# First chunk's copies on ScalarE and its keys turned ahead of the queries' product; VectorE scales queries ahead of the settling

## The chip, the cores and the metric

The kernel runs on one core of a Trainium2 chip. The metric is device time in microseconds; lower is better. A core has TensorE (matrix products, PE in the profile), VectorE (DVE), ScalarE (ACT), GpSimd (POOL) and SyncE (SP). Each engine works through its own queue in order. TensorE's results land in PSUM, eight banks of 128 x 512 float32.

## The reference, cut to what matters

A block with layer norm, an attention that has a sparse and a local part, and a small product with rounded operands, on a batch of 4 sequences of 1024 tokens of 512 channels, 16 heads of 128:

```
xn  = layernorm(x)
q   = rope(rmsnorm(xn @ Wq + bq));  lk = rope(rmsnorm(xn @ Wlk + blk));  lv = xn @ Wlv + blv
ck, cv = compressed keys and values: each 4 tokens pooled by softmax(xn @ Wcmp), then @ Wk, @ Wv
sparse: softmax over the top 8 of the causal q.ck, times cv
local:  softmax over q.lk of this window of 128 and the one before, times lv
out = x + (0.5 * (sparse + local)) @ Wo + bo + fp8(xn) @ fp8(input2) rescaled
```

All of the attention is float32.

## The kernel before, in words

A chunk is 128 tokens (one window); there are 32 chunks, `t` = 0 to 31, eight to a batch element (c = 0 to 7). A unit is two heads of a chunk: eight units to a chunk, `u` = 0 to 7, and 256 units in all. One loop goes over stages, `for s in range(-3, NN + 2)`, and each stage works on several units at once, as a pipeline written out by hand; the order of the calls in the loop is the order of the instructions in every engine's queue (the schedule is manual). In stage `s`:

- `scores(s)`: TensorE, local and sparse scores of both heads into two PSUM banks (`sc`).
- `keep_context(s-2)`: ScalarE copies the context out of PSUM (`cT`, L779).
- `weigh(s)`: VectorE finds the minimum, the top 8 and marks them (L649 to L655), ScalarE takes the exponentials (L656, L664).
- `queries(s+3)`: TensorE, the product for queries and local keys of a unit (`qp`, L478), two banks.
- `turn_keys_here(s+1)`: TensorE turns scaled queries and keys (`tq`, L534), only in the first chunk. Later chunks turn them by VectorE transposes and DMAs through memory (`turn_keys`, L556, L559, L564, and `fetch_keys`, L574).
- `settle(s)`: VectorE zeroes what is not in the top 8 and divides (L671, L680, L681, L682). `settle_window(s)`: ScalarE divides the local part (L687).
- `normalize(s+2)`: VectorE scales queries and keys out of PSUM (`th`, L506), GpSimd and VectorE begin the rotary embedding (`rotate`: `rb`, L332 on GpSimd, and L333 on VectorE). `end_rotation(s+2)` finishes it (L335, L336).
- `turn(s)` and `fetch(s)`: the probabilities are transposed on VectorE (L705), written to memory (L713) and read back turned (`probT`, L747). In the first chunk and for the last unit TensorE turns them instead (`turn_here`, L728) and `keep_turned` copies them out of PSUM (L736).
- `squares(s+3)` on ScalarE (L318) and `spread(s+3)` on GpSimd (L312, L313: the factor `r` that `normalize` of the next stage needs).
- `keep_keys(s+1)`: in the first chunk, copies `tq` to `qT` (L540) and `lkT` (L541).
- `to_output(s-2)` (L797), `values_of(s+1)` (`vp`, L581), `values(s-1)` (`cp`, L764): TensorE. `keep_values(s+1)`: ScalarE copies `vp` to `lv` (L593).

Between these stand `steps()`, twice a stage: pieces of `chunk_prep(t+2)` (layer norm, `xn`, its transposes `xp`, copies `xnT`, the product `yp`, the compressed entries `ep`, `kv`, their rotation `rb_e`, `ckT`) and of `chunk_eight(t)` (rounding of the chunk, L284 to L295, and its product `fp`).

Only in the first chunk: at the end of stages 0 to 7 `fold_first_row(s)` changes a unit's query weights in place on VectorE (`wqk`, L269) after a DMA (`load_first_row`), stages 0 to 3 also round `w2` on VectorE and GpSimd (`round_w2`), and ScalarE's queue issues DMAs for weights.

SyncE's queue issues, in each later stage: the write of the probabilities, four writes of the keys (L564, after L559), four reads of the turned probabilities (L747), two reads of the turned keys (L574). Two PSUM banks, tag `pp`, are used in turn by `tq`, `vp`, `tp` and the tiles of the chunk's preparation (`xp`, `yp`, `ep`, `cp` for `ckT`, `fp`), so a new tile waits until the one before the last has been copied out.

Of the kernel before, what the change touches and what calls it, by code (L numbers as in the profile page):

```python
# [12 lines left out]
F32 = mybir.dt.float32  # L13
BF16 = mybir.dt.bfloat16
U32 = mybir.dt.uint32
AF = mybir.ActivationFunctionType
ALU = mybir.AluOpType
AX = mybir.AxisListType

P = 128  # L20
# [18 lines left out]
def kernel(  # L39
# [26 lines left out]
    nc = tc.nc  # L66
    B, S, HID = hidden.shape
# [10 lines left out]
    work = ctx.enter_context(tc.tile_pool(name="work", bufs=2))  # L78
# [7 lines left out]
    def scratch(name, shape=(P, 512), dtype=F32):  # L86
        return work.tile(list(shape), dtype, tag="scratch", name=name, bufs=2)

    def pp(name):
        return psum.tile([P, 512], F32, tag="pp", name=name, bufs=2)  # L90
# [229 lines left out]
    def rotate(th, cs, nh, a, name):  # L320

        p = th.shape[0]
        a = a.rearrange("p (h t f) -> p h t f", h=nh, t=2)
        bb = work.tile([p, nh, 2, HALF], F32, tag=f"ropeb{nh}", name=f"rb_{name}", bufs=1)
        x12 = th[:, :, 0:ROPE].rearrange("p h (t f) -> p h t f", t=2)

        def wide(v):
            return v.unsqueeze(1).unsqueeze(1).to_broadcast([p, nh, 2, HALF])  # L330

        nc.gpsimd.tensor_tensor(bb, x12, wide(cs[:, HALF:ROPE]), ALU.mult)  # L332
        nc.vector.tensor_tensor(a, x12, wide(cs[:, 0:HALF]), ALU.mult)  # L333
        yield
        nc.vector.tensor_tensor(x12[:, :, 0, :], a[:, :, 0, :], bb[:, :, 1, :], ALU.subtract)  # L335
        nc.vector.tensor_tensor(x12[:, :, 1, :], a[:, :, 1, :], bb[:, :, 0, :], ALU.add)  # L336
# [5 lines left out]
    def chunk_prep(t):  # L342

        b, c = divmod(t, NCH)
        xt = x_tiles.pop(("norm", t))
        if c == 0:
            entries[b] = (
                work.tile([P, 2 * P], F32, tag="ckT", name=f"ckT_{b}"),
                work.tile([P, 2, D], F32, tag="cv", name=f"cv_{b}"),
            )  # L350
        ckT, cv = entries[b]
        st = work.tile([P, 8], F32, tag="lnst", name=f"lnst_{t}")
        nc.vector.bn_stats(st[:, 0:6], xt)
        nc.vector.bn_aggr(st[:, 6:8], st[:, 0:6])
        r = rstd_of(st[:, 7:8], 1, 1.0, EPS_LN, f"lnr_{t}")
        yield "A0"
        if c == 0:
            nc.gpsimd.memset(cv, 0.0)
        yield "B0"

        off = work.tile([P, 2], F32, tag="off", name=f"off_{t}")
        nc.gpsimd.tensor_scalar(off[:, 0:1], st[:, 6:7], -1.0, None, ALU.mult)
        nc.scalar.activation(
            xt, xt, AF.Identity, bias=off[:, 0:1], scale=1.0, accum_out=off[:, 1:2]
        )
        nc.gpsimd.tensor_scalar(off[:, 1:2], off[:, 1:2], 1.0 / HID, None, ALU.mult)
        yield "A1"
        xn = scratch(f"xn_{t}")
        nc.vector.tensor_scalar(xn, xt, off[:, 1:2], r, ALU.subtract, ALU.mult)
        yield "B1"  # L370
        xp = pp(f"xp_{t}")
        for k in range(KK):
            nc.tensor.transpose(xp[:, ts(k, P)], xn[:, ts(k, P)], ident)  # L373
        yield "A2"
        xnT = work.tile([P, KK + 1, P], F32, tag="xnT", name=f"xnT_{t}")
        nc.scalar.copy(xnT[:, 0:KK, :].rearrange("p k s -> p (k s)"), xp)
        if t:
            nc.scalar.copy(xnT[:, KK, :], xp[:, 0:P])
            nc.vector.memset(xnT[0:1, KK, :], 1.0)
        chunks[t] = xnT  # L380
        yield "B2"


        yp = pp(f"yp_{t}")
        for k in range(KK):
            nc.tensor.matmul(  # L386
                yp[:, 0 : 2 * D + 1],
                xnT[:, k, :],
                wkv_sb[:, k, :],
                start=(k == 0),  # L390
                stop=(k == KK - 1),
            )
        yield "A3"
        y = scratch(f"y_{t}")[:, 0 : 2 * D + 1]
        nc.scalar.copy(y[:, 0 : 2 * D], yp[:, 0 : 2 * D])
        nc.gpsimd.memset(y[:, 2 * D : 2 * D + 1], 1.0)
        nc.vector.tensor_scalar(
            logits[:, 0:1], yp[:, 2 * D : 2 * D + 1], bcmp_sb, None, ALU.add
        )
        row = work.tile([P, 2, BLK], F32, tag="row", name=f"row_{t}", bufs=1)  # L400
        red = work.tile([P, BLK // RATIO], F32, tag="red", name=f"red_{t}", bufs=1)
        nc.vector.transpose(row[:, 0, :], logits)
        fours = row[:, 0, :].rearrange("p (n r) -> p n r", r=RATIO)
        nc.vector.tensor_reduce(red, fours, AX.X, ALU.max)
        nc.vector.tensor_tensor(
            fours, fours, red.unsqueeze(2).to_broadcast([P, BLK // RATIO, RATIO]), ALU.subtract
        )
        nc.scalar.activation(row[:, 0, :], row[:, 0, :], AF.Exp)
        yield "B3"
        yield "A4"  # L410
        spread_w = work.tile([P, NE], F32, tag="spread", name=f"spread_{t}", bufs=1)
        nc.vector.transpose(row[:, 1, :], row[:, 0, :])
        nc.vector.tensor_scalar(spread_w, picks, row[:, 1, 0:1], None, ALU.mult)
        yield "B4"
        ep = pp(f"ep_{t}")
        nc.tensor.matmul(ep[0:NE, 0 : 2 * D + 1], spread_w, y, start=True, stop=True)  # L416
        yield "A5"
        total = work.tile([NE, 1], F32, tag="total", name=f"total_{t}", bufs=1)
        kv = work.tile([NE, 2, D], F32, tag="kv", name=f"kv_{t}", bufs=1)
        nc.vector.reciprocal(total, ep[0:NE, 2 * D : 2 * D + 1])  # L420
        nc.vector.scalar_tensor_tensor(
            kv.rearrange("p h d -> p (h d)"),
            ep[0:NE, 0 : 2 * D],
            total,
            bkv_sb,
            ALU.mult,
            ALU.add,
        )
        yield "B5"
        g, o = divmod(c * NE, P)  # L430
        nc.scalar.copy(cv[o : o + NE, g, :], kv[:, 1, :])
        ess = work.tile([NE, 1], F32, tag="ess", name=f"ess_{t}", bufs=1)
        square_sum(ess, kv[:, 0, :], f"e{t}")
        er = rstd_of(ess, 1, 1.0 / D, EPS_RMS, f"er_{t}")
        ck = kv[:, 0:1, :]
        yield "A6"
        nc.vector.scalar_tensor_tensor(
            ck[:, 0, :], ck[:, 0, :], er, norm_w[0:NE, 1, :], ALU.mult, ALU.mult
        )
        ra = work.tile([NE, ROPE], F32, tag="ra_e", name=f"ra_e{t}", bufs=1)  # L440
        for _ in rotate(ck, angles[t][1], 1, ra, f"e{t}"):
            pass
        yield "B6"
        cp = pp(f"cp_{t}")
        nc.tensor.transpose(cp[:, 0:NE], ck[:, 0, :], ident[:NE, :NE])  # L445
        yield "A7"
        nc.vector.tensor_copy(ckT[:, ts(c, NE)], cp[:, 0:NE])
        yield "B7"
# [18 lines left out]
    units = {}  # L467
# [33 lines left out]
    def normalize(n):  # L501
# [15 lines left out]
        next(w["rotation"])  # L517
        w["th"], w["thb"] = th, thb

    def end_rotation(n):  # L520
        for _ in units[n].pop("rotation"):
            pass
# [13 lines left out]
    def keep_keys(n):  # L536
        w = units[n]
        tq = w.pop("tq").rearrange("p (t g a i) -> p t g a i", t=2, g=2, a=NB)
        qT, lkT = key_tiles(n)
        nc.scalar.copy(qT.rearrange("p a (i g) -> p g a i", g=2), tq[:, 0])  # L540
        nc.vector.tensor_copy(lkT.rearrange("p a (g i) -> p g a i", g=2), tq[:, 1])  # L541

    def key_tiles(n):
        w = units[n]
# [144 lines left out]
    def parts_of(n):  # L689

        c, m, _, _ = columns(n)
        return range(0 if c else 1, 3 if m <= P else 4)
# [38 lines left out]
    def keep_turned(n):  # L731
        w, g = units[n], len(parts_of(n))
        probT = work.tile([P, 1024], F32, tag="probT", name=f"probT_{n}", bufs=1)
        probT = of_heads(probT, n)
        for h, tp in enumerate(w.pop("tp")):
            (nc.vector.tensor_copy if h else nc.scalar.copy)(  # L736
                probT[:, :, ds(h * g, g), :],
                tp.rearrange("p (g a i) -> p a g i", a=NB, i=BLK),
            )
        w["probT"] = probT  # L740
# [81 lines left out]
    def for_unit(n, *todo):  # L822
        if 0 <= n < NN:
            for f, *more in todo:
                f(n, *more)
# [9 lines left out]
    for s in range(-3, NN + 2):  # L835
        t, u = place(s)
# [10 lines left out]
        for_unit(s, (scores, 0), (scores, 1))  # L847
        for_unit(s - 2, (keep_context,))
        for_unit(s, (weigh, 0), (weigh, 1))
        for_unit(s + 3, (queries,))  # L850
        if s + 1 < NU:
            for_unit(s + 1, (turn_keys_here,))
        for_unit(s, (settle, 0), (settle, 1))
        for_unit(s, (settle_window, 0), (settle_window, 1))
        for_unit(s + 2, (normalize,))
        if by_dma(s):
            turn(s)
        if s < 0:
# [92 lines left out]
```

## Time and profile before

| | |
|---|---|
| median of 4 runs | 2797.93 us (2797.27 to 2799.34) |
| the profiled execution: time, span | 2797.12 us, 2795.4 us |
| TensorE busy | 2732.9 us (98%) |
| VectorE busy | 2264.9 us (81%) |
| ScalarE busy | 1345.2 us (48%) |
| GpSimd busy | 843.1 us (30%) |
| first scores of unit 0, 1, ... 8 at | 45.13, 59.29, 76.78, 91.42, 109.88, 125.31, 137.56, 149.51, 158.72 us |

All times are from one profiled execution, in microseconds from the start of its span. A line of the timeline gives the start, the time, the engine, the line of the kernel, the operation, what it writes and reads, shapes, a count, and in brackets how long the engine stood idle before it and what ended that. A line of the waits gives who waited for whom, the total, how many times, and the longest. TensorE's clock is the granted one, 1.00 for full.

The stages of the first chunk (from one unit's first scores to the next's) take 9.2 to 18.5 us; those of the later chunks take 8.8 to 12.4 us.

### The profile page before, as it was taken

The page shows a single profiled execution, that of the slowest core. Times are in us where ns is not written, and L with a number is a line of the kernel's source. Part 1 is how long each engine was busy: PE and PEld are TensorE (multiplying, and loading weights), DVE is VectorE, ACT ScalarE, POOL GpSimd, SP SyncE. Part 2 cuts the span into 40 slices and gives each one's busy share as a digit, 9 for nine tenths or more (in the row PEclk, how much of TensorE's full clock was granted, in tenths as well). Part 3 has the DMA queues.
Part 4 walks back from the last instruction along what each step waited for, and adds up shares of the span by engine and source line. Part 5 has one row for each costly group of instructions (what it writes and reads, how often), then busy time and mean ns, then how long its engine had stood idle before and what let it go on. Part 6 is the DMA issues. An engine that isn't in the chain of part 4 may idle for free.

```text
span 2795.4 us, 48431 instructions
## 1 busy us (share of the span) xinstructions
PE 2732.9 (98%) x12686; PEld 1855.6 (66%) x12721; DVE 2264.9 (81%) x9171; ACT 1345.2 (48%) x5170; POOL 843.1 (30%) x1225
## 2 busy tenths in 40 slices
PE   5799999999999999999999999999999999999998
PEld 3566666676666666666666666666666666676665
DVE  4687888888877788888887787888888878888887
ACT  2344554544455554444445555444444555444543
POOL 2333332233232333322233322333223333222331
PEclk8899999999999999999999999999999999999999
DMA  6244445555544445555554444555555444455554
GB/s 203 93 124 138 135 137 152 159 152 152 148 126 141 139 137 143 151 154 155 148 144 132 134 139 138 154 154 144 153 150 142 128 138 140 135 155 161 147 148 128
DMA packets 623187, 401.96 MB, mean 144 GB/s; under 512 B 307152, under 2 KB 576320, under 8 KB 622912
## 3 DMA queue, kind: packets, MB, share of 16 engines
q1 hardware_dynamic: 610688, 385.29, 49.7%
q10 hardware_dynamic: 12224, 13.56, 1.5%
q8 instruction: 104, 1.70, 0.3%
q14 instruction: 171, 1.40, 0.2%
HBM read 214.64 MB, written 184.03 MB: 143 GB/s over the span
## 4 chain that ended last, share of the span: by engine, by line
PE 93%; DVE 2%; DMA 0%; issue 0%; ACT 0%; SPq 0%; POOL 0%; DVEq 0%; ACTq 0%
PE qp L478 31%; PE op L797 15%; PE vp L581 15%; PE cp L764 14%; PE sc L626 5%; PE sc L616 4%; PE sc L623 4%; PE yp L386 2%; PE fp L458 1%; PE ep L416 1%; PE xp L373 0%; DVE wqk L269 0%; PE sc L627 0%; DMA probT<-pr 0%; PE cp L445 0%
## 5 line engine op out<-in xcount | busy, mean ns | idle before, releaser
L478 PE MATMUL qp<-wqk,xnT 128*128 128x512 f32 x2048 | 945.4, 604 | 2.8 <-issue 2.1
L332 POOL TENSOR_TENSOR rb<-th,cs 128x256 f32<-128x256 f32 x256 | 248.5, 971 | 1674.7 <-DVE th L506 1674.7
L478 PEld LDWEIGHTS qp<-wqk,xnT 128*128 128x128 f32 x2048 | 370.6, 191 | 383.4 <-issue 372.3
L581 PEld LDWEIGHTS vp<-wlv,xnT 128*128 128x128 f32 x2048 | 393.0, 192 | 181.2 <-issue 115.3
L581 PE MATMUL vp<-wlv,xnT 128*128 128x256 f32 x2048 | 491.3, 383 | 17.5 <-DVE lkT L541 13.6
L656 ACT ACTIVATE prob<-sc,neg 128x256 f32<-128x256 f32 (+1 forms) x512 | 235.5, 460 | 553.6 <-DVE taken L655 543.9
L797 PE MATMUL op<-wo,cT 128*128 128x512 f32 x1024 | 488.0, 599 | 0.5 <-ACT cT L779 0.5
L649 DVE CUSTOM_DVE_ANT_0 sc<-sc,mask_b 128x256 f32<-128x256 f32 (+1 forms) x512 | 208.4, 407 | 277.9 <-PE sc L627 277.7
L593 ACT COPY lv<-vp 128x256 f32<-128x256 f32 x256 | 95.2, 372 | 469.7 <-PE cp L764 410.7
L687 ACT ACTIVATE prob<-prob,tot 128x256 f32<-128x256 f32 (+1 forms) x512 | 252.4, 493 | 129.0 <-DVE tot L681 127.7
L797 PEld LDWEIGHTS op<-wo,cT 128*128 128x128 f32 x1024 | 186.4, 190 | 189.4 <-issue 128.0
L764 PE MATMUL cp<-probT,lv 128*128 128x128 f32 x1920 | 299.8, 276 | 6.1 <-DMA probT<-pr 5.3
L318 ACT ACTIVATE junk<-qp 128x128 bf16<-128x128 f32 x1024 | 279.7, 273 | 33.0 <-PE qp L478 4.9
L506 DVE SCALAR_TENSOR_TENSOR th<-qp,r,norm_w 128x128 f32<-128x128 f32 x1024 | 287.0, 343 | 7.4 <-PE tq L534 4.1
L764 PEld LDWEIGHTS cp<-probT,lv 128*128 128x128 f32 x1920 | 274.7, 192 | 22.7 <-issue 10.5
L705 DVE STREAM_TRANSPOSE probB<-prob 128x512 f32<-128x512 f32 (+2 forms) x494 | 282.2, 609 | 0.0
L313 POOL TENSOR_TENSOR r<-r,nhalf 128x4 f32<-128x4 f32 x256 | 260.6, 1018 | 21.3
L764 PE MATMUL cp<-probT,cv 128*128 128x128 f32 x1536 | 256.6, 276 | 0.0
L626 PE MATMUL sc<-ckT,qT 128*128 128x96 f32 (+7 forms) x1024 | 226.5, 303 | 0.0
L764 PEld LDWEIGHTS cp<-probT,cv 128*128 128x128 f32 x1536 | 214.1, 193 | 0.0
L623 PE MATMUL sc<-lkT,qT 128*128 128x128 f32 x1024 | 208.1, 285 | 0.0
L779 ACT ACTIVATE cT<-cp,blvT 128x128 f32<-128x128 f32 x512 | 160.0, 364 | 91.6 <-PE cp L764 82.3
(130 smaller groups left out, 3797.0 us busy)
## 6 DMA issues: line engine op xcount, KB each, us to landing
pr<-probB SPq DMA_DIRECT2D x127, 512.0 KB, 2.6
probT<-pr SPq DMA_DIRECT2D x508, 128.0 KB, 2.9
qk<-thb SPq DMA_DIRECT2D x992, 64.0 KB, 1.8
pr<-probB SPq DMA_DIRECT2D x96, 384.0 KB, 2.3
probT<-pr SPq DMA_DIRECT2D x384, 96.0 KB, 2.3
qT<-qk SPq DMA_DIRECT2D x248, 128.0 KB, 2.9
lkT<-qk SPq DMA_DIRECT2D x248, 128.0 KB, 2.7
x_norm<-_attn_hidden_states_dram SPq DMA_DIRECT2D x32, 256.0 KB, 3.2
```

The lines of the kernel that those rows point to most:

```text
L313: nc.gpsimd.tensor_tensor(r, r, nhalf[: ss.shape[0], 0:n], ALU.pow)
L318: nc.scalar.activation(junk[: src.shape[0]], src, AF.Square, accum_out=acc)
L332: nc.gpsimd.tensor_tensor(bb, x12, wide(cs[:, HALF:ROPE]), ALU.mult)
L478: nc.tensor.matmul(qp, xnT[:, k if k or not t else KK, :], wqk_sb[u][:, k, :], start=(k == 0), stop=(t > 0 and k == KK - 1),)
L506: nc.vector.scalar_tensor_tensor(th[:, i, :], qp[:, ts(i, D)], r[:, i : i + 1], norm_w[:, i // 2, :], ALU.mult, ALU.mult,)
L581: nc.tensor.matmul(vp[:, 0:256], xnT[:, k, :], wlv_sb[u][:, k, :], start=(k == 0), stop=(k == KK - 1),)
L623: nc.tensor.matmul(blocks(sc[:, P : 2 * P]), q, lkT[:, :, ds(h * BLK, BLK)], start=True, stop=True)
L626: nc.tensor.matmul(sc[:, spa], q, ckT[:, 0:m], start=True, stop=False)
L687: nc.scalar.mul(prob[:, loc], prob[:, loc], tot[:, 0:1])
L705: nc.vector.transpose(pb[:, :, ds(h * g, g), :], prob[:, parts[0] * P : (parts[-1] + 1) * P].rearrange("p (g b i) -> p b g i", b=NB, i=BLK),)
L764: nc.tensor.matmul(blocks(cp[:, h, :]), v, probT[:, :, h * len(parts) + i - parts[0], :], start=(i == parts[0]), stop=(i == parts[-1]),)
L797: nc.tensor.matmul(op, cT[:, h, :], wo_sb[u][:, h, :], start=(u == 0 and h == 0), stop=(u == NU - 1 and h == 1),)
```

## The change

Six edits:

1. `chunk_prep(0)` no longer centres the chunk on ScalarE; VectorE subtracts the mean of the statistics directly. Later chunks keep the centring.
2. `rotate` yields once more, between GpSimd's and VectorE's first products, and a new call `go_on_rotating` continues it.
3. `keep_keys`: the copy to `lkT` goes from VectorE to ScalarE.
4. `keep_turned`: the second head's copy goes from VectorE to ScalarE.
5. `turn_keys_here(s+1)` goes ahead of `queries(s+3)`.
6. `normalize(s+2)` (scaling and GpSimd's part of the rotation) goes ahead of `settle(s)`, and VectorE's first part of the rotation stays behind `settle_window(s)`.

```diff
@@ rotate
         nc.gpsimd.tensor_tensor(bb, x12, wide(cs[:, HALF:ROPE]), ALU.mult)
+        yield
         nc.vector.tensor_tensor(a, x12, wide(cs[:, 0:HALF]), ALU.mult)
         yield
@@ chunk_prep
-        off = work.tile([P, 2], F32, tag="off", name=f"off_{t}")
-        nc.gpsimd.tensor_scalar(off[:, 0:1], st[:, 6:7], -1.0, None, ALU.mult)
-        nc.scalar.activation(
-            xt, xt, AF.Identity, bias=off[:, 0:1], scale=1.0, accum_out=off[:, 1:2]
-        )
-        nc.gpsimd.tensor_scalar(off[:, 1:2], off[:, 1:2], 1.0 / HID, None, ALU.mult)
+        xn = None
+        if t:
...
+        else:
+            xn = scratch(f"xn_{t}")
+            nc.vector.tensor_scalar(xn, xt, st[:, 6:7], r, ALU.subtract, ALU.mult)
         yield "A1"
-        xn = scratch(f"xn_{t}")
-        nc.vector.tensor_scalar(xn, xt, off[:, 1:2], r, ALU.subtract, ALU.mult)
+        if t:
+            xn = scratch(f"xn_{t}")
+            nc.vector.tensor_scalar(xn, xt, off[:, 1:2], r, ALU.subtract, ALU.mult)
         yield "B1"
@@
+    def go_on_rotating(n):
+        next(units[n]["rotation"])
+
@@ keep_keys
-        nc.vector.tensor_copy(lkT.rearrange("p a (g i) -> p g a i", g=2), tq[:, 1])
+        nc.scalar.copy(lkT.rearrange("p a (g i) -> p g a i", g=2), tq[:, 1])
@@ keep_turned
-            (nc.vector.tensor_copy if h else nc.scalar.copy)(
+            nc.scalar.copy(
@@ the loop over stages
         for_unit(s, (weigh, 0), (weigh, 1))
-        for_unit(s + 3, (queries,))
         if s + 1 < NU:
             for_unit(s + 1, (turn_keys_here,))
+        for_unit(s + 3, (queries,))
+        for_unit(s + 2, (normalize,))
         for_unit(s, (settle, 0), (settle, 1))
         for_unit(s, (settle_window, 0), (settle_window, 1))
-        for_unit(s + 2, (normalize,))
+        for_unit(s + 2, (go_on_rotating,))
         if by_dma(s):
             turn(s)
```

## The prediction

> **What bounds the kernel now.** I read the busy times by stretch first, then the waits of each engine inside and outside the first chunk, then the timeline of single stages.
>
> ```profile
> 45.00:159.00 114.00, 88.67 (x370) 59.98 (x373) 79.96 (x286) 39.51 (x171) 40.62 (x46) 0.90 0.40 124
> 190.00:2780.00 2590.00, 2582.64 (x12085) 1758.51 (x12113) 2139.30 (x8718) 1277.65 (x4894) 776.87 (x1125) 1.00 0.52 145
> ```
>
> The columns are stretch, length, busy PE, PEld, DVE, ACT, POOL, then clock. From 190 us on TensorE is full, so that nothing is won there; only a late feed can lose. The first chunk's eight stages (45 to 159) leave TensorE idle for 25 us and run it at a mean clock of 0.90. So gain and loss have separate places. What TensorE waits for, before 185 us and after:
>
> ```profile
> PE vp L581 <- DVE lkT L541: 13.6, 4, 5.3
> PE tp L728 <- DVE lkT L541: 10.2, 3, 4.5
> ...
> PE cp L764 <- DMA probT<-pr: 3.6, 2, 2.2
> ```
>
> In the first chunk it waits for the key copy `lkT`, which frees the `pp` bank for the next product. The timeline of stage 6 (scores at 137.56) shows why that copy is late:
>
> ```profile
> 137.76 0.37 ACT L736 COPY probT<-tp 128x256 f32<-128x256 f32 x1 [3.87 <-PE cp L764]
> 138.16 0.42 DVE L736 COPY probT<-tp 128x256 f32<-128x256 f32 x1 [3.32 <-ACT probT L736]
> 138.50 2.28 DVE L269 TENSOR_TENSOR wqk<-wqk,first_row 128x2048 f32<-128x2048 f32 x1
> 140.70 0.29 DVE L649 CUSTOM_DVE_ANT_0 sc<-sc,mask_b 128x128 f32<-128x128 f32 x1
> ```
>
> VectorE idles 3.32 us for ScalarE's half of a copy out of the same bank, and only then folds the weights (2.28) while the scores, ready at about 138.2, wait until 140.70. In later chunks the last feed is the fetch of the turned probabilities, tightest in the seventh stage of a chunk (u=6); here in the last chunk of a batch:
>
> ```profile
> 755.33 1.82 SPq L747 DMA_DIRECT2D probT<-pr  x4
> 759.98 0.68 PE L764 MATMUL cp<-probT,lv 128*128 128x128 f32 x4
> ```
>
> The last issue ends at 757.15, and the product that reads it starts 2.83 later, already 0.13 behind its usual place.
>
> **First chunk: the gain.** With both copies on ScalarE VectorE's idle before the fold goes: the fold runs inside it, and the scores are taken up about 0.65 after the scores' first product (X) instead of 3.2 to 4.5. ScalarE pays one copy more, but back to back its copies start 0.27 apart (L736 to L593 at 137.76 and 138.03).
>
> The new chain from the first read of scores (w), by the rows of stage 6: weighing 1.71, queries 1.15 (now in front), settling to the second reciprocal 1.28, to its L687 0.26, to the squares 0.31, four squares 1.45, two key copies 0.68: 6.85. With what GpSimd holds up (below, 0.47) it is 7.32. After the key copy come the four turns and the values, 0.05+0.44+0.90 = 1.39, or 3.11 where one more `pp` tile (xp, yp, ep, cp of the chunk's preparation) puts `vp` behind the copy too: stages 0, 1, 3, 5. TensorE alone needs 1.02+0.44+3.73+1.72+1.72+0.44+0.90 = 9.97.
>
> - Stage 0: ScalarE issues DMAs until 50.63, as now: 14.16 becomes 14.0.
> - Stages 1 to 4 have the rounding of `w2` on GpSimd across the settling, which now costs 0.93 (L671) and 1.03 (L680); after the move L295 and then `rb` stand there: 1.85, 1.55, 1.65, 1.45. They are bounded by what now shows (1.96) and by L295 alone (1.26). Stage 1: VectorE waits in stage 0 for the second chunk's `xnT` (10.9), rotates 0.6, folds 2.28, rounds 1.34, all by 15.1, so w is 1.1: 1.1+6.85+1.85+3.11 = 12.9 (17.49 now). Stage 2: it waits for `y` (10.2), then logits 0.8, rotation 0.5, fold, rounding, w 2.2: 12.0 (14.64). Stage 3: no such wait, w 1.35: 13.0 (18.46). Stage 4: w 0.65, and 0.8 for ScalarE's `cv` and square of `kv`: 11.15 (15.43).
> - Stage 5: the rotation of `kv` waits for GpSimd until 10.8 of stage 4, the fold ends at X+2.65: 2.7+7.32+3.11 = 13.1 (12.25): a loss.
> - Stage 6: 9.97 (11.95). Stage 7: 9.35 (9.21).
>
> Two covers: ScalarE's four DMA issues ahead of the exponentials of stages 1 and 2 (2.05) are hidden by the scaling that VectorE now does first, else they cost 0.6 each. And the turn, now ahead of the queries' product on TensorE, needs the bank that the copy of `lv` frees: two copies and this one end at about X+0.95, TensorE comes to it at 1.02; if later, the product waits as long.
>
> That is 95.5 for 113.6: 18.1 saved. Stages 1 and 3 are also short because `vp` no longer runs slowly: after an idle time of 5.30 it took 3.78 for 1.89, while after 2.08 TensorE was at full pace. Stage 5 leaves 3.0 idle; between 2.08 and the 3.60 that slowed it (89.08) I take full pace, else 1.7 is lost. The Trainium skill, TensorE: Matmul & The Clock Gate (Part 1, the HAM clock gate), puts the idle window at about 3.4 us; by it stage 5 stays fast too, and a miss of 0.4 there would cost that 1.7.
>
> **Start.** Without the centring the first chunk's `xn` needs no ScalarE pass: `xnT` moves from 13.36 to 10.43, where the table load ends. But the turn of unit 0 now stands ahead of the third query product and waits for the rotation (29.4, now 26.5), so this product starts at 27.45 against 27.24. The gain comes from the next scaling, which waited 4.05 for that turn: `kv` ends at about 33.6 against 35.62. I take 2.0; bounds 0 (weights late) to 2.9. The fold of unit 7 and its followers come earlier, which removes TensorE's 1.76 before 179.64: 1.7. The last stage's second copy, now behind the first on ScalarE, delays `cT` there: -0.3. Sum of gains 21.5; by the doubtful stages 14 to 26.
>
> **All later stages: the loss.** The queries are scaled ahead of the settling, so GpSimd's `rb` starts as the settling does. Two rows of now:
>
> ```profile
> 84.85 1.26 POOL L295 TENSOR_TENSOR w_sb<-wo 128x512 bf16<-128x512 f32 x1
> 84.93 1.20 DVE L680 TENSOR_SCALAR tot<-tot 128x2 f32<-128x2 f32 x1
> ...
> 748.10 0.42 DVE L333 TENSOR_TENSOR thb<-th,cs 128x256 f32<-128x256 f32 x1
> 748.15 0.97 POOL L332 TENSOR_TENSOR rb<-th,cs 128x256 f32<-128x256 f32 x1 [7.81 <-DVE th L506]
> ```
>
> L680 normally takes 0.17; under a GpSimd instruction it lasts until that one ends. `rb` alone would take 0.72 (by 1.265 for 512 columns and 0.31 for `rb_e`'s 64); it shows 0.97 because L333 holds it 0.25. Behind it today are transposes, which show no delay; the second half of the rotation (L333, 0.42) only changes its place. After the change they are L671, then L680: `rb` ends about 1.02 after L671 starts, L680 would start at 0.46 and gets through some 0.1 before the end: 0.46; with 32 columns 0.82-0.23-0.1 = 0.49. I take 0.47 per stage, bounds 0 and 0.72.
>
> The Trainium skill, SBUF — State Buffer (Who interferes with whom), speaks against the change: VectorE with two SBUF inputs or in a two-port mode and GpSimd lock each other out for whole instructions. Taken whole it makes 0.41+0.72-0.46 = 0.67, and the loss below about 12 us larger.
>
> Most stages hide 0.47: VectorE idles about 1.7 before the next scores. Two in each chunk don't. In u=5 the rotation of `kv` goes through GpSimd behind `r`:
>
> ```profile
> 739.04 1.01 POOL L313 TENSOR_TENSOR r<-r,nhalf 128x4 f32<-128x4 f32 x1
> 740.03 0.31 POOL L332 TENSOR_TENSOR rb_e<-kv,cse 32x64 f32<-32x64 f32 x1
> 740.37 0.18 DVE L335 TENSOR_TENSOR kv<-ra_e,rb_e 32x32 f32<-32x32 f32 x1 [1.23 <-POOL rb_e L332]
> ```
>
> `r` waits for ScalarE's squares, these for L687, which now comes 1.15+0.47 = 1.62 later; of that 0.84 is taken up by waits of now (squares end at 737.90, `r` starts at 738.61 and is held 0.16): L335 is 0.78 late. VectorE goes into u=6 without idle, adds 0.47: its last transpose, the eight SyncE issues behind it and the probabilities are 1.25 late. In a batch's first chunk, 0.57 is taken up: 1.52. Against this, the time from the last issue's end to the product in u=6, chunk 0 to 7: 2.53, 3.32, 3.00, 2.71, 3.16, 2.98, 2.91, 2.83. Needed are 2.83 where it binds (128 KB, 2.9 to landing), 2.23 for 96 KB (2.3), 2.07 for 64 KB (2.1). Spare: 0.46, 1.05, 0.73, 0.44, 0.33, 0.15, 0.08, 0, mean 0.40. Mean lateness 1.38 less 0.40 is 0.98, in 30 chunks (1 to 30; the last has no preparation): 29 us.
>
> **Sum.** The profiled execution took 2797.12 (span 2795.4 and 1.7 around it), 0.8 under the median. 2797.12-21.5+29 = 2804.6; on the median 2805.
>
> **Rivals.** *Faster, 2780:* `rb` finds the port free and VectorE loses nothing. Lateness is then 0.31 to 0.58, only chunks 0 and 4 to 7 stall, 4 us in all: 2797.9-21.5+4. The point is a hold of 0.34 a stage (mean lateness 0.445+2x, less 0.40, times 30, equals 21.5); under it the change wins. For it: the four scalings read PSUM, and a two-column L680 may slip in ahead. Against: L680's 1.20. *Even, 2797:* a hold of 0.3 with the gain as worked out: loss 19. *Worse, 2818:* the first chunk gives only 8, as `vp` stays at half pace and the fold waits for `first_row` (4.97 once). For it: DMA share 0.40 in this stretch, with queues shared. That the edits do nothing at the start (weights late) changes only 2 us.
>
> **How the numbers follow.** Slower as forecast 0.40, faster rival 0.35, even 0.17, worse 0.08. A measurement here tells about 0.2% (5.6 us) from none. Even gives 0.04 to faster and 0.11 to same (the rest to slower); the forecast's own range, 2798 to 2814, gives 0.09 to same. Faster 0.39, same 0.20, slower 0.41. The range 2780 to 2816 leaves out the worse rival and the faster one's tail.
>
> **What will show it.** Scores of unit 8 at about 138.5 (now 158.72); no VectorE wait at `probT`; L680 of the first head at 0.6 instead of 0.17; TensorE's wait for `probT` in u=6 near 1 us a chunk. Wrong if L680 stays at 0.17, or if that wait stays under 10 us in all.

## The result, and the profile after

The change makes no difference that can be told: median 2797.02 us (34 runs, 2793.58 to 2801.30) against 2798.53 (52 runs), ratio 0.9995 with a 95% interval of 0.9991 to 1.0000. The profiled execution has a span of 2793.2, 2.2 less than before. The gain and the loss of the forecast are both there, and they cancel: the gain was larger than I had it, the loss smaller.

Busy times by stretch of the kernel after (columns as before):

```profile
45.00:159.00 114.00, 103.04 (x473) 68.29 (x476) 95.14 (x357) 57.58 (x239) 52.63 (x60) 0.99 0.50 148
190.00:2780.00 2590.00, 2566.30 (x11965) 1740.45 (x11994) 2182.45 (x8623) 1280.32 (x4846) 723.77 (x1118) 1.00 0.54 143
```

In the first stretch TensorE is busy for 103 us instead of 89, at a clock of 0.99 instead of 0.90, and gets through ten stages in place of eight. In the long stretch it idles 23.7 us instead of 7.4. TensorE's waits up to 160 us (us in total, times, longest):

```profile
PE vp L591 <- ACT lkT L551: 6.2, 2, 4.0
PE tp L738 <- ACT lkT L551: 2.7, 2, 1.5
```

The two waits for the key copy were 23.8 and are 8.9. Behind 160 us:

```profile
PE cp L774 <- DMA probT<-pr: 16.0, 21, 2.2
```

From 190 us on it is 16.0 too, and it was 3.6 before. It grew by 12.4, half of what the later stages lose in the table below: the row counts a wait only from the modelled end of the matmul before, and the product usually starts 0.16 ahead of that end. By their lengths, the stages that hold the products of u=5 and u=6 grew by 23.1 in chunks 1 to 30.

Stage 6 in the timeline (scores at 112.41, columns start and duration) shows the first mechanism; the fold ahead of it is stage 5's:

```profile
109.59 2.29 DVE L269 TENSOR_TENSOR wqk<-wqk,first_row 128x2048 f32<-128x2048 f32 x1
...
112.61 0.37 ACT L746 COPY probT<-tp 128x256 f32<-128x256 f32 x1 [1.64 <-PE cp L774]
112.88 0.38 ACT L746 COPY probT<-tp 128x256 f32<-128x256 f32 x1
113.02 0.30 DVE L659 CUSTOM_DVE_ANT_0 sc<-sc,mask_b 128x128 f32<-128x128 f32 x1 [1.14 <-PE sc L637]
```

VectorE no longer waits for a copy: the fold is over at 111.88, before the scores exist, and they are taken up 0.61 after their first product instead of 3.14. The last rows answer to u=5 and u=6 of chunk 7 (stages from 704.13, 714.83 and 725.91):

```profile
714.66 1.01 POOL L313 TENSOR_TENSOR r<-r,nhalf 128x4 f32<-128x4 f32 x1
715.65 0.31 POOL L332 TENSOR_TENSOR rb_e<-kv,cse 32x64 f32<-32x64 f32 x1
715.99 0.18 DVE L336 TENSOR_TENSOR kv<-ra_e,rb_e 32x32 f32<-32x32 f32 x1 [1.82 <-POOL rb_e L332]
...
731.20 1.82 SPq L757 DMA_DIRECT2D probT<-pr  x4
735.88 0.68 PE L774 MATMUL cp<-probT,lv 128*128 128x128 f32 x4 [0.89 <-DMA probT<-pr]
```

From its stage's start, `r` begins 0.63 later than before (10.53 for 9.90), the last issue of u=6 ends 0.89 later (18.19 for 17.30), and the product 2.86 behind it waits the same 0.9.

By the starts of the stages the difference of 2.2 comes apart so:

| part | before | after | difference |
|---|---|---|---|
| start, to the scores of unit 0 | 45.13 | 40.34 | -4.8 |
| first chunk, units 0 to 7 | 113.59 | 90.88 | -22.7 |
| stage 9 | 12.18 | 10.18 | -2.0 |
| unit 10 to unit 255 | 2593.60 | 2618.93 | +25.3 |
| tail | 20.74 | 22.71 | +2.0 |

### The profile page after: what moved, and what is told of

Its sections match the earlier page's. It is cut to its first block, busy times and chain, and to the rows that moved or that the text cites. A ratio compares the mean times of both kernels' runs of the same rounds, so it can differ in the third digit from the quotient of the medians.

```text
span 2793.2 us, 48833 instructions
## 1 busy us (share of the span) xinstructions
PE 2736.0 (98%) x12686; PEld 1848.8 (66%) x12721; DVE 2320.2 (83%) x9154; ACT 1364.4 (49%) x5185; POOL 795.9 (28%) x1223
## 5 line engine op out<-in xcount | busy, mean ns | idle before, releaser
L332 POOL TENSOR_TENSOR rb<-th,cs 128x256 f32<-128x256 f32 x256 | 193.7, 756 | 1025.9 <-DVE th L513 1025.9
L313 POOL TENSOR_TENSOR r<-r,nhalf 128x4 f32<-128x4 f32 x256 | 265.5, 1037 | 21.3
L690 DVE TENSOR_SCALAR tot<-tot 128x2 f32<-128x2 f32 x512 | 195.4, 382 | 17.7
L312 POOL TENSOR_SCALAR r<-ss 128x4 f32<-128x4 f32 x256 | 60.2, 235 | 517.4 <-ACT junk L318 512.2
```

Source lines behind the costliest of these rows:

```text
L313: nc.gpsimd.tensor_tensor(r, r, nhalf[: ss.shape[0], 0:n], ALU.pow)
```

## The experiments

Times in brackets are the stretch from unit 10 to unit 255 in the profiled execution. It took 2593.6 to 2596.2 in the six versions with the old order there (mean 2595.1).

**1. Early scaling in the first chunk alone.**

```diff
+        early = s < NU
+        if early:
+            for_unit(s + 2, (normalize,))
         for_unit(s, (settle, 0), (settle, 1))
         for_unit(s, (settle_window, 0), (settle_window, 1))
+        if not early:
+            for_unit(s + 2, (normalize,))
         for_unit(s + 2, (go_on_rotating,))
```

> The kernel after, but from the second chunk on the queries are scaled behind the settling again, as before the change. Theory: the change's gain lies in the start and the first chunk, and its loss, 25 us by the stage starts of its trace (27.5 us ahead at unit 8, 2.0 more in stage 9, 4.2 ahead at unit 255), all comes from scaling ahead of the settling in later chunks; then unit 255 is reached 25 us earlier and the median is about 2772 (2768 to 2775), L690 of the first head lasts 0.17 again and TensorE's wait for probT falls from 16 us to under 5. Rival: the loss is a fixed backlog that a quicker first chunk leaves for the later ones (fetches and weights that come no earlier); then it stays, and the median is 2795 to 2798.

Measured: 2773.94, ratio 0.9909 (0.9895 to 0.9922). This version beats both kernels. TensorE's wait is gone:

```profile
PE cp L774 <- DMA probT<-pr: 0.9, 3, 0.4
```

And the settling's second instruction is no longer held (the group of L690: busy us, mean ns of one, idle before; first this version, then the kernel after):

```profile
L690 DVE TENSOR_SCALAR tot<-tot 128x2 f32<-128x2 f32 x512 | 92.4, 180 | 17.8
```

```profile
L690 DVE TENSOR_SCALAR tot<-tot 128x2 f32<-128x2 f32 x512 | 195.4, 382 | 17.7
```

**2. The same edit alone, in the later chunks alone, on the kernel before** (`early = s >= NU`).

> The kernel before, with one edit alone, in the later chunks alone: from the second chunk on the queries are scaled ahead of the settling and rotated on behind it. The first chunk is as before. Theory: the loss of 25 us is this edit's and does not need the quick first chunk: about 2823 (2819 to 2828). Rival: it is a backlog of the quick first chunk: 2798 to 2801.

Measured: 2823.76, ratio 1.0086 (1.0072 to 1.0100); the first chunk took 114.0 as before, the later stretch 2618.8. The loss is this edit's, and needs no quick first chunk. TensorE's wait, counted here up to 2796 us of a span of 2821.8 (15.7 over the whole span):

```profile
PE cp L768 <- DMA probT<-pr: 13.5, 22, 1.6
```

**3. Old order in u=5 and u=6 alone** (`early = s < NU or u not in (5, 6)`).

> The kernel after, but in the later chunks the queries are scaled behind the settling again in the two stages u=5 and u=6 alone; the other six stages of a chunk keep the new order. Theory: in the other stages VectorE's idle before the next scores hides the hold, so these two carry the whole loss: 2770 to 2775, TensorE's wait for probT under 5 us. Rival: every stage loses its share, six of eight stay: 2797 less a quarter of 25 is about 2791.

Measured: 2774.91, ratio 0.9911 (0.9898 to 0.9925), [2596.8]; the wait for `probT` was 5.4. In six stages of eight the early scaling costs at most the 1.7 us above the mean, though VectorE is held in these too.

**4. `rb` written behind the settling.** `rotate` yields ahead of GpSimd's product instead of behind it.

> The kernel after, but from the second chunk on GpSimd's product rb starts behind the settling, while VectorE's four scalings stay ahead of it. Theory: the loss needs the port hold; without it L690 of the first head lasts 0.17 again, the settling moves by the scalings' 1.15 alone, of which 0.84 is taken up by waits in u=5, so that about 0.3 of lateness is left there and the wait for probT falls to under 5 us in all: 2772 to 2778. Rival: the order alone makes the loss, as the squares come behind later windows and r behind rb: rb now ends later and r and rb_e behind it, so the wait stays at 12 us or more: 2790 to 2800.

Measured: 2798.31, ratio 0.9996 (0.9987 to 1.0004). Neither theory was tested, since the edit changed nothing: the place in the code did not order the two engines here. GpSimd had no work ahead of `rb` and started it when `th` was there, as in the kernel after:

```profile
1305.42 0.80 POOL L334 TENSOR_TENSOR rb<-th,cs 128x256 f32<-128x256 f32 x1 [5.69 <-DVE th L516]
1305.68 0.57 DVE L693 TENSOR_SCALAR tot<-tot 128x2 f32<-128x2 f32 x1
```

**5. `rb` made to wait.** As 4, but GpSimd first copies something that the settling writes:

```diff
     def go_on_rotating(n):
+        if n - 2 >= NU:
+            seen = work.tile([P, 2], F32, tag="seen", name=f"seen_{n}")
+            nc.gpsimd.tensor_copy(seen, heads[n - 2, 1]["tot"])
         next(units[n]["rotation"])
```

> The kernel after, but from the second chunk on GpSimd first copies two columns of the second head's settled tot and only then runs rb, so that rb really starts behind the settling; the four scalings stay ahead of it. Theory (hold and order add up): L690 of the first head is back at 0.17, the settling moves by about 0.9 instead of 1.34; u=5 is then 0.1 to 0.3 late and u=6 no more than that, of which a mean of 0.40 is spare: TensorE's wait for probT is 2 to 6 us in all, the median 2776 to 2781. Rival (order alone makes the loss): the wait stays at 12 us or more and the median at 2788 or above.

Measured: 2776.60, ratio 0.9921 (0.9909 to 0.9934), [2599.6]. Now `rb` comes behind the second head's reciprocal, and the wait falls from 16.0 to 5.6:

```profile
1299.26 0.17 DVE L697 RECIPROCAL tot<-tot 128x2 f32<-128x2 f32 x1
...
1299.56 0.28 POOL L533 COPY seen<-tot 128x2 f32<-128x2 f32 x1 [7.94 <-DVE tot L697]
...
1299.80 0.92 POOL L334 TENSOR_TENSOR rb<-th,cs 128x256 f32<-128x256 f32 x1
```

```profile
PE cp L780 <- DMA probT<-pr: 5.6, 6, 1.9
```

With the scaling still early, 19 of the 24 us are back. The order alone costs about 4.5.

**6. The hold alone.** Version 1, with a GpSimd product of `rb`'s size under the settling of every later stage, whose result nobody reads:

```diff
+        pad = work.tile([P, 4, 2, HALF], F32, tag="ropeb4", name=f"pad_{n}", bufs=1)
...
+        nc.gpsimd.tensor_tensor(pad, ..., cs..., ALU.mult)
```

> The version with the old order in the later chunks (2774), and in each of their stages one more GpSimd product of rb's size and shape on norm_w, whose result nobody reads, started when the second head's taken is there, so that it runs under the settling. It is the port hold without the moved scaling. Theory: L690 is held by about 0.4 again, u=5 takes it up in its waits, u=6 gets 0.4 late against a mean spare of 0.40: 3 to 6 us lost, 2777 to 2780. Rival (the hold alone makes the loss): 2788 or above. Third case (order alone): 2774 to 2776.

Measured: 2791.12, ratio 0.9970 (0.9959 to 0.9981), [2611.1]; the rival's range came, and the hold alone makes 16.0 of the 23.9. My theory's slip can be read in the trace: the waits that take up 0.84 in u=5 lie ahead of `r`, behind the squares. In the old order `rb` stands between the settling and the `kv` rotation, so that the hold is passed on: in u=5 of chunk 14 `rb` starts 0.56 later than in the kernel before, `r` (L313) 0.50 and the end of the `kv` rotation 0.49. GpSimd's own time is not what delays them: the added product ends 2.87 before `rb` starts there. The held instruction starts 0.04 behind the product and lasts to its end:

```profile
1301.70 0.72 POOL L532 TENSOR_TENSOR pad<-norm_w,cs 128x256 f32<-128x256 f32 x1
1301.74 0.71 DVE L702 TENSOR_SCALAR tot<-tot 128x2 f32<-128x2 f32 x1
```

**7 and 8. `rb` made to wait in u=5 alone, and in u=6 alone** (the edit of 5, with `(n - 2) % NU == 5` or `6` as a further condition).

> The kernel after, but in u=5 of the later chunks alone GpSimd waits for the settled tot before rb, so that the hold is gone there and stays in the other stages. Theory (what is late in u=5 is added to what is late in u=6): the turned probabilities of u=6, 1.07 late on the mean, come back to about 0.68, and by the versions with 0.20, 0.72 and 1.07 of lateness (3, 15 and 23 us lost) that loses about 14 of the 23 us: 2786 to 2790. Rival (u=5's waits hide its hold, u=6 alone decides): 2794 to 2798.

> The same with u=6 of the later chunks alone: the hold is gone there and stays in u=5 and the others. Theory (they add up): lateness 1.07 becomes about 0.65, 2785 to 2790. Rival (u=6 alone decides): nearly the whole loss goes, 2775 to 2780.

Measured: u=5 2784.69, ratio 0.9955 (0.9942 to 0.9969), [2606.2]; u=6 2787.65, ratio 0.9962 (0.9949 to 0.9974), [2608.3]. Against the kernel after that is 12.3 and 9.4 us: the two holds add up, to 21.7 for the 20.4 that experiment 5 brought. TensorE's waits, u=5 first:

```profile
PE cp L780 <- DMA probT<-pr: 11.2, 13, 2.5
```

```profile
PE cp L780 <- DMA probT<-pr: 10.0, 12, 2.4
```

How late the versions are against the kernel before (means over chunks 2 to 30, from each stage's start; end of the last transpose in u=5, end of `probB`'s transposes in u=6), and what the later stretch loses against 2595.1:

| version | u=5 late | u=6 late | lost |
|---|---|---|---|
| 5, order without hold | 0.44 | 0.22 | 4.5 |
| 7, hold not in u=5 | 0.43 | 0.65 | 11.2 |
| 8, hold not in u=6 | 0.86 | 0.65 | 13.2 |
| 6, hold without order | 0.39 | 0.76 | 16.0 |
| after | 0.86 | 1.09 | 23.9 |

The loss goes with how late u=6's probabilities are turned. Lateness in u=5 has a smaller price of its own, in the stages u=6 that read what u=5 fetched: in chunks 1 to 30 they grew by 5.0 and 6.5 in the two versions with 0.86, and by 0.7 to 1.1 in the three with about 0.4.

**9 to 11. The copies of the first chunk.** On the kernel before: both on ScalarE (edits 3 and 4), only the keys' (3), only the second head's probabilities (4).

> The kernel before with the two copies of the first chunk (keys, and turned probabilities of the second head) on ScalarE, and nothing else. Theory: VectorE's wait of 20.6 us for ScalarE's half of probT and of 6.3 for its half of the keys is what made the weights' fold and the scores late: 12 to 18 of the first chunk's 22.7 us come back, 2781 to 2787. Rival: the turn ahead of the queries' product is what feeds the key copy early, and the copies alone give under 6: 2793 to 2798.

> The kernel before with the first chunk's key copy lkT on ScalarE, and nothing else. Theory (the root is VectorE's wait for ScalarE's half of probT, 20.6 us, which puts the fold and the next scores late): this copy alone shortens only the end of the chain, 3 to 8 us, 2792 to 2797. Rival (the root is where lkT stands: VectorE comes to it late, and TensorE waits 23.8 us for it in all): 14 us or more, 2786 or below.

> The kernel before with the first chunk's second copy of turned probabilities on ScalarE, and nothing else. Theory: the 20.6 us wait is the root, the fold starts that much earlier, and 15 to 20 us of the two copies' 24 come back: 2780 to 2785. Rival (the place of lkT is the root): under 10 us, 2790 or above.

Measured: both 2775.53, ratio 0.9912 (0.9898 to 0.9925); keys 2792.85, 0.9979 (0.9970 to 0.9987); probabilities 2780.78, 0.9937 (0.9925 to 0.9950). So 24.3, 5.7 and 17.8 us: the two add up, and two moved copies bring nearly what version 1 brings (25.7). For both together the theory had too little, for each alone it held. VectorE's largest wait from 45 to 160 us (20.6 in all before) stays when the keys' copy alone moves:

```profile
DVE probT L736 <- ACT probT L736: 19.1, 6, 5.0
```

TensorE then waits on for the key copy, though it now stands on ScalarE, since the scores it hangs on are still late:

```profile
PE vp L581 <- ACT lkT L541: 13.3, 3, 5.1
PE tp L728 <- ACT lkT L541: 8.3, 3, 4.3
```

**12. No early scaling anywhere** (the kernel after without edit 6).

> The kernel after without edit 6 anywhere: the queries are scaled behind the settling in every stage, the first chunk's too; the copies on ScalarE, the turn ahead of the queries' product and the first block without centring stay. Theory: on the first chunk's chain from the first read of scores to the key copies the scaling only adds 1.15 and the hold 0.4, so without it stages 1 to 5 get shorter by up to 1 us each: 2768 to 2773. Rival: the early scaling is part of the gain, since it fills the wait for the exponentials and covers ScalarE's DMA issues: 2777 to 2785.

Measured: 2775.21 (2769.29 to 2777.07), ratio 0.9909 (0.9896 to 0.9923): the same as version 1, so neither theory. It is also the same as version 9 (2775.53), so that edits 1 and 5 show no gain that can be told on top of the two copies. The first chunk took 90.7 for version 1's 91.0. Stages 1, 2 and 4 are 0.6 to 0.7 shorter each, as I had it, but stage 3 is 1.3 longer, and stage 9 1.1. In stage 3 `vp` stands behind the key copy here, as in the kernel before, and 3.21 lie behind that copy; in version 1 it is 1.91 (the next section says why).

## Why the prediction was wrong

The likeliest case, slower by 7.5, did not come. 2797 was inside the range and is the number of the rival *Even*, but it came by luck, not by that rival's numbers (hold 0.3, loss 19, gain 21.5): the hold was 0.40 to 0.44, the loss 24, the gain 26 (2799.59 to 2773.94). The two mechanisms and their places were right; the sum failed at two terms of the same sign.

- *Scores of unit 8 at 138.5.* They came at 131.22. Right in kind (158.72 before), 7 short.
- *No VectorE wait at `probT`, w of 0.65.* Right: 0.61 in stage 6, and the copies alone take the first chunk from 113.6 to 92.2, 21.4 of the 22.7.
- *First chunk 95.5.* It took 90.88. Stages 0 to 7 were 14.0, 12.9, 12.0, 13.0, 11.15, 13.1, 9.97, 9.35 in the forecast and 13.66, 12.68, 11.55, 11.85, 11.24, 11.09, 9.61, 9.20 in the trace. **The step that failed** is the 3.11 behind the key copy in stages 3 and 5: I put `vp` behind that copy wherever the preparation takes one more `pp` tile. From the copy's end to the next scores it was 3.51 and 3.21 in stages 0 and 1, but 1.92 and 1.44 in stages 3 and 5, so that the term was 2.9 too long, of 4.6 in all. In stage 3 `vp` starts 0.10 behind the read of `ep` (by the times; the profile names no release), in stage 5 behind the copy of `ckT`, both ahead of the key copy:

```profile
86.38 0.47 DVE L428 SCALAR_TENSOR_TENSOR kv<-ep,total,bkv_sb 32x256 f32<-32x256 f32 x1
86.95 1.97 PE L591 MATMUL vp<-wlv,xnT 128*128 128x256 f32 x8 [1.04 <-issue]
87.78 0.38 ACT L551 COPY lkT<-tq 128x256 f32<-128x256 f32 x1
...
109.23 1.99 PE L591 MATMUL vp<-wlv,xnT 128*128 128x256 f32 x8 [0.83 <-DVE ckT L454]
...
110.58 0.39 ACT L551 COPY lkT<-tq 128x256 f32<-128x256 f32 x1
```

  In the kernel before, `vp` did stand behind the key copy in stage 5:

```profile
133.92 0.42 DVE L541 COPY lkT<-tq 128x256 f32<-128x256 f32 x1 [0.49 <-ACT qT L540]
134.26 0.18 DVE L447 COPY ckT<-cp 128x32 f32<-128x32 f32 x1
134.40 1.99 PE L581 MATMUL vp<-wlv,xnT 128*128 128x256 f32 x8 [1.22 <-DVE lkT L541]
```

  It started 0.04 ahead of the end of the copy of `ckT`. So the two `pp` banks are not taken strictly in turn, as the description of the kernel has it: `vp` could take the bank of either tile, and the forecast carried the one of the kernel before over to a kernel in which the other is read first. How the bank is chosen stays open: in stage 3 of version 12 `vp` went with the key copy though `ep` had been read 0.16 earlier. Stage 5, forecast as a loss, was a gain.
- *Start 2.0, stage 9 1.7.* 4.8 and 2.0 in this execution. The nine versions with the new start reached unit 0 at 42.1 on the mean, the five with the old one at 44.6: 2.5. Part of that is TensorE's pace in these single executions (last section): where the third query product was fast it is 40.6 (five versions) against 43.0 (version 9 alone), where it was slow 44.0 against 45.0 (four each). So the start brought 1.0 to 2.4, and some 3 of the 4.8 are luck. What the dropped centring brings by itself was not tried.
- *L680 of the first head at 0.6, a hold of 0.47.* Right: the group's mean is 382 ns for 180, which is 0.40 on every first head if none falls on the second; in the first chunk a row shows the whole of it:

```profile
106.74 0.73 POOL L332 TENSOR_TENSOR rb<-th,cs 128x256 f32<-128x256 f32 x1 [5.74 <-DVE th L513]
106.80 0.69 DVE L690 TENSOR_SCALAR tot<-tot 128x2 f32<-128x2 f32 x1
```

  The Trainium skill, SBUF — State Buffer (Who interferes with whom), lets the later instruction block for the whole of the earlier one. The rows agree: L690 ends with `rb`, here and in experiment 6. How much of `rb` was left made the price, and the 0.67 that I had drawn from that page did not come.
- *u=5 late by 0.78 to 1.05.* Right: 0.86. The hold makes half of it (0.86 against 0.44 without).
- *u=6 "adds 0.47", so 1.25 to 1.52 late.* **The other failing step.** 1.09 was measured against a forecast mean of 1.38 (that of two chunks, taken for all eight): u=6 added 0.23. The hold did add its 0.44 (1.09 against version 8's 0.65), but the early scaling gives 0.21 back: in version 5, which has it without the hold, `probB` was turned 0.21 earlier in u=5 than before. Part of it: in u=5 of chunk 14 the four scalings take 1.16 up to the next instruction where the rotation follows (version 1) and 1.03 where the settling does (version 5). At 1.09 the forecast's own formula, less 0.40 and times 30, gives 21 instead of 29.
- *The wait in u=6 near 1 us a chunk.* Stages u=7, where that wait falls, grew by 18.1 in 30 chunks, 0.60 each. A further 5.0 came in stages u=6, for u=5's own fetch: I had left that out, as its issues too stand behind the transposes that are 0.86 late.
- *Tail -0.3.* It took 2.0 longer, at a mean clock of 0.88 instead of 1.00. That is not the edit's: with the same last stage it took 20.8 in version 12 (clock 1.00) and 23.0 in version 1 (0.93).

By the medians the gain was 4 short and the loss 5 too high, which is the way from 2805 to 2797.

## What to carry to other kernels

Where an edit is good in one stage of a loop and dear in another, split it by stage before you weigh the sum: the version that scales early in the first chunk alone was 0.9% faster, and the two moved copies alone were as fast. A GpSimd instruction that is moved beside a chain on VectorE should be looked at for what it holds. To keep it off that chain it took a real dependence here; the place where it is written did nothing. When a step is said to wait for a buffer, read which tile's release it took in a neighbouring stage before a constant is put on all of them.

## What was not expected of the hardware

With the turn ahead of the queries' product, TensorE waits in the start for the rotation of unit 0, and then goes on at full pace or at about half. Nine versions have this start. With waits of 0.53, 2.40, 2.67, 2.74 and 3.06 us the third product kept full pace and unit 0's scores began at 40.2 to 41.0. With 3.11, 3.35, 3.36 and 4.34 the pace was lost and they began at 43.6 to 44.3. The closest pair, version 8 and then version 4 (four turns, and the first matmul of the product, which takes 1.8 times as long):

```profile
26.64 0.63 PE L550 MATMUL tq<-ident,th 128*128 128x128 f32 x4 [3.06 <-DVE th L340]
27.10 0.59 PE L488 MATMUL qp<-wqk,xnT 128*128 128x512 f32 x1
```

```profile
27.07 1.09 PE L547 MATMUL tq<-ident,th 128*128 128x128 f32 x4 [3.11 <-DVE th L340]
27.95 1.06 PE L488 MATMUL qp<-wqk,xnT 128*128 128x512 f32 x1
```

It is no fixed length of the wait: with the old start, a wait of 2.09 left the third product slow in the kernel before (5.37), and 2.10 left it fast in version 9 (3.67). So the forecast's "after 2.08 TensorE was at full pace" was no safe bound in its own trace. The granted clock shows what differs. In all 14 traces it changes only at multiples of 3.41 us from its first change, and where these steps lie differs from one execution to the next. For version 8, then version 4 (columns as in the prediction, PE busy first behind the length, clock third from the end):

```profile
21.57:24.98 3.41, 2.00 (x6) 0.58 (x4) 1.82 (x7) 1.30 (x8) 1.91 (x3) 1.00 1.10 348
24.98:28.39 3.41, 1.75 (x7) 1.07 (x8) 1.47 (x5) 0.26 (x2) 2.22 (x5) 1.00 1.01 311
28.39:31.81 3.42, 3.08 (x9) 0.99 (x7) 1.82 (x7) 0.00 (x0) 1.12 (x2) 1.00 0.95 317
```

```profile
22.69:26.11 3.42, 1.27 (x4) 0.29 (x2) 2.51 (x8) 1.47 (x8) 1.76 (x2) 1.00 1.05 271
26.11:29.52 3.41, 2.45 (x6) 1.58 (x7) 1.27 (x6) 0.00 (x0) 2.10 (x4) 0.50 0.97 323
```

In version 4 most of the wait fell into one step, in which TensorE was busy for 1.27, and the clock of the next was 0.50. In version 8 the wait lay across the end of a step; each part was busier, and the clock stayed. Up to about 33 us of the 14 traces the clock fell behind every step with at most 1.32 busy and stayed full behind every one with at least 1.58; of the three between, one fell. The Trainium skill, TensorE: Matmul & The Clock Gate (Part 1, the HAM clock gate), tells of a free-running window, so that the same program can fall on either side; these rows agree with that better than with a fixed idle time of about 3.4 us.
